# The end of a layer 3 block done in 256-column pieces over the next block's items, with its projection in the bank of the sums, and query evacuations shared by two engines

## The chip, the cores and the metric

The kernel runs on one core of one Trainium2 chip. The metric is the device time of the whole program in microseconds, the median of the timed runs. All data are fp32.

## The reference

Four layers follow each other on an activation `x` of shape (4, 64, 64, 64): four images of 64 x 64 positions (N = 4096) with 64 channels.

```
layer 0: q, k, v = x Wq + bq, x Wk + bk, x Wv + bv         # (B, 4096, 64)
         attn = softmax(q k^T)                              # over j of energy[i, j]
         x = gamma * (attn^T v) + x
layer 1: y = LN(x); y = pointwise 64 -> 256; depthwise 3x3; y1 * y2; channel scale; pointwise 128 -> 64
         x = x + y * beta;  z = LN(x); pointwise 64 -> 256; z1 * z2; pointwise 128 -> 64;  x = x + z * gamma
layer 2: xf = x as (B, 64, 4096), rows are one image axis
         x = softmax(xf^T xf) applied to xf, added to x
layer 3: g, phi, theta = x gW, x phiW, x thetaW             # (B, 4096, 32)
         y = softmax(theta phi^T) g;  w = y W + b           # (B, 4096, 64)
         x = x + gamma * (w - mean(w)) / sqrt(var(w) + eps) + beta   # mean, var over B, H, W
```

## The kernel before

The fast path (`fast_path`) keeps the four images in SBUF as one tile `X` and makes every softmax without a maximum: exps of scores with a constant shift, and sums beside them. At the end `check_sums` (L1635 on) counts whether all sums lie in a safe range and writes a flag; if it is not zero, a general path computes everything again. With the inputs of the reference the flag is zero and only the fast path runs.

The work is written as a list of **items**. An item is a function that issues the scores and exps of one step of the main stream; `at(i, fn)` (L936) puts a function into the list `due` of item i, where it runs after the item's own function. So each engine gets its instructions in the order in which this program is walked through (`run`, L1495 on), and works them off in that order; TensorE, ScalarE and VectorE (here DVE) are under a manual schedule. Beside the items run two **lanes**, `conv` (layer 1 of an image, beside the main stream of later ones) and `misc` (projections, loads, features). A lane is a generator: each `yield us` states after how many us of the main stream's estimated time (3.6 an item of layer 0, 4.6 of layer 2, 1.0 of layer 3) its next piece is issued. The lane's pieces thus fall between items, at places that these numbers set.

The order of the main stream is: layer 0 of images 0 to 3; layer 2 of image 0; then layer 2 of image b followed by layer 3 of image b - 1; at last layer 3 of image 3 directly after layer 3 of image 2.

**Buffers.** `ps` has three PSUM tiles of two banks (128 x 1024) in rotation; all scores, projections and lane products go through them. `acc` has two PSUM tiles of one bank (128 x 512): in layer 3 one holds y, the other (`accz`) the sums z. `e` has six SBUF tiles of 128 x 2048 for the exps, `t` two of 128 x 1024.

**Layer 3** (`layer3`, L1349 on). An image has two blocks (nb = 0, 1) of 2048 queries, and each block has 32 items, one for each 128 keys (mc). In item n:

- `scores(n)`: eight matmuls (L1361) with 32 rows and 64 columns of the array each fill two `ps` tiles, and ScalarE's two exps (L1367) turn them into e(n), 128 x 2048.
- two items later `products(n)`: four matmuls (L1389) add to y in `acc`. The sums of the exps are taken in two ways. In most items DVE adds e(n) to `esum` (L1385; L1383 for the first pair). At mc = 9, 19 and 29 TensorE instead multiplies e(n) by ones into z (four matmuls, L1378). At mc = 31 ScalarE copies y to `yz` (L1395), after both exps that were issued before it.
- two items after that `totals(nb)`: `sums` (L1399) adds esum to z on TensorE; ScalarE makes 1/z as exp(-ln z) (L1410, L1411, 512 columns each); DVE refines it by one Newton step and multiplies y by it (L1412 to L1414).
- four items later `close(nb)`: `project` (L1419) multiplies y by the output weights, four matmuls into a `ps` tile; one ScalarE instruction of 1024 columns adds the bias into `wy` (L1432); DVE takes the batch statistics (L1434).

In the last block of all, `close_last` (L1436 on) does this in halves of 256 columns, with lines L1440 to L1456 in place of those. For the second block of images 0 and 1, whose next items are those of layer 2, `totals` comes directly after the last product.

The features of layer 3 (`open3`: L1315 and its DVE evacuation L1319, L1325 and L1329, L1340 and L1342) and the last scaling of layer 2 (`close2`, L1291 to L1298) run in the misc lane; for image 3 they fall into layer 3 of image 2, its first block.

**Layers 0 to 2.** Layer 0's scores are L1031 with exps L1036, its products L1056, which DVE adds up (L1063). In layer 2 they are L1245, L1253 and L1262. `project0(b)` makes queries and values of the next image within layer 0: for images 1 to 3 (`once`) four matmuls (L982) fill a `ps` tile whose two partition halves DVE evacuates, one after the other, with the bias added (L990, 64 x 1024 each); values go through L1007 and L1009. `norm` (L1077 on) is layer 1's layer norm: ScalarE squares x (L1082), a yield of 4.0, then TensorE sums x and the squares over the channels (L1088). `features2` transposes X for layer 2 (L1224) into a `ps` tile that DVE and ScalarE evacuate (L1227).

**The end.** `finish` computes the batch statistics' scale and shift and stores eight parts of the output. Before the last part's two copies (L1630 on DVE, L1631 on ScalarE) and its store it issues `check_sums`.

## Time and profile before

The device time is 2654.44 us, the median of 3 runs (2654.04 to 2654.82). The profiled execution has a span of 2652.8 us, at a granted TensorE clock of 0.997.

| stretch | what runs | time |
|---|---|---|
| image 0's first layer 3 block | 32 items | 70.88 us |
| image 2's first layer 3 block | 32 items, and image 3's features | 78.38 us |
| image 2's second layer 3 block | 32 items, and the end of the block before | 73.01 us |
| image 3's first layer 3 block | 32 items, and the end of the block before | 73.02 us |

| operation | engine | time of one |
|---|---|---|
| exp of 128 x 1024 (L1367) | ScalarE | 1022 ns |
| add of 128 x 2048 (L1385) | DVE | 2292 ns |
| Ln, Exp of 512 columns (L1410, L1411) | ScalarE | 613, 630 ns |
| bias add of 1024 columns (L1432) | ScalarE | 1133 ns |
| q evacuation of 64 x 1024 (L990) | DVE | 1284 ns |

A busy TensorE in this profile is one with a matmul in flight. Several matmuls on different parts of the array run side by side, so the duration of one says little: a step's cost is read from start to start in the timeline. In a group's line, the numbers after the bar are the busy time in all, the mean of one in ns, and the idle time of the engine just before them with what ended it. In the table by stretch, each engine has its busy time and number of instructions, in the order PE (matmul), PEld (weight load), DVE, ACT (ScalarE), POOL; the last three are the clock, the share of the DMA engines and their GB/s. A timeline line has start, duration, engine, line, operation, and in brackets the idle time before it and what ended it.

### The profile page before, as it was taken

What the parts mean: (1) busy time and instruction counts of PE and PEld (TensorE: products, weight loads), DVE (VectorE), ACT (ScalarE), POOL (GpSimd) and SP (SyncE); (2) the same over time, 40 slices, a digit from 0 to 9 for tenths busy, and PEclk for the clock granted to TensorE, in tenths of its full rate; (3) what the DMA queues carried; (4) which work ended last, traced back from release to release, by engine and by line L of the source; (5) the groups of instructions that cost most, each with busy time, mean ns of one, the idle gap of its engine ahead of it and who ended that gap; (6) DMA issues with size and microseconds to landing.
All of it is one profiled execution on the core that took longest, in us unless ns stands there. A gap on an engine that the chain in (4) does not pass through costs nothing.

```text
span 2652.8 us, 50797 instructions
## 1 busy us (share of the span) xinstructions
PE 2612.8 (98%) x22421; PEld 830.2 (31%) x22421; DVE 1348.6 (51%) x1555; ACT 1718.6 (65%) x2787; POOL 16.4 (1%) x66
## 2 busy tenths in 40 slices
PE   8999999999999999999999999999999999999998
PEld 3333233333323323333333322243322333322223
DVE  3232386633876338621672148800068600098997
ACT  4555655656566565666656668756578755578886
POOL 2000000000000000000000000000000000000000
PEclk9999999999999999999999999999999999999999
DMA  3000000001000100010010000010000010010002
GB/s 73 1 17 1 17 8 10 1 17 25 9 1 1 32 17 1 1 33 17 1 33 17 17 1 1 2 33 1 17 1 2 1 33 1 1 33 2 1 1 66
DMA packets 24282, 36.46 MB, mean 14 GB/s; under 512 B 3725, under 2 KB 12150, under 8 KB 24054
## 3 DMA queue, kind: packets, MB, share of 16 engines
q1 hardware_dynamic: 23141, 32.03, 5.5%
q8 instruction: 178, 2.92, 0.5%
q0 software_dynamic: 672, 0.56, 0.1%
q10 hardware_dynamic: 240, 0.54, 0.1%
q14 instruction: 51, 0.41, 0.1%
HBM read 4.80 MB, written 4.19 MB: 3 GB/s over the span
## 4 chain that ended last, share of the span: by engine, by line
PE 93%; DVE 4%; ACT 2%; issue 0%; DMA 0%; SPq 0%; DVEq 0%; ACTq 0%
PE acc L1056 17%; PE acc L1262 17%; PE ps L1031 17%; PE ps L1245 16%; PE ps L1361 10%; PE acc L1389 8%; PE ps L1118 2%; DVE tg L1385 2%; PE accz L1378 1%; ACT e L1253 1%; PE ps L1209 1%; PE ps L1186 1%; PE ps L1088 1%; PE ps L1340 1%; PE ps L1007 0%
## 5 line engine op out<-in xcount | busy, mean ns | idle before, releaser
L1036 ACT ACTIVATE e<-ps 128x1024 f32<-128x1024 f32 x512 | 517.1, 1025 | 338.1 <-PE ps L1031 225.8
L1253 ACT ACTIVATE e<-ps 128x1024 f32<-128x1024 f32 x512 | 517.0, 1025 | 305.0 <-PE ps L1245 304.9
L1367 ACT ACTIVATE e<-ps 128x1024 f32<-128x1024 f32 x512 | 496.0, 1022 | 85.4 <-PE ps L1361 78.3
L1385 DVE TENSOR_TENSOR tg<-tg,e 128x2048 f32<-128x2048 f32 x214 | 490.4, 2292 | 24.7 <-ACT e L1367 5.7
L1031 PE MATMUL ps<-X,q 64*64 64x512 f32 x4096 | 475.5, 599 | 7.6 <-DVE q L990 4.1
L1245 PE MATMUL ps<-ko 64*64 64x512 f32 x4096 | 469.8, 591 | 2.2 <-ACT ko L1227 1.6
L1262 PE MATMUL acc<-e,X 64*64 64x512 f32 x4096 | 468.5, 591 | 2.6 <-DVE inv L1412 1.6
L1056 PE MATMUL acc<-e,vq 128*64 128x512 f32 x2048 | 467.4, 598 | 0.0
L1063 DVE SCALAR_TENSOR_TENSOR yv<-acc,gam,yv 128x512 f32<-128x512 f32 x224 | 167.8, 750 | 322.6 <-PE acc L1056 311.7
L1157 DVE SCALAR_TENSOR_TENSOR y<-pad,vec,y 128x1024 f32<-128x1024 f32 x240 | 308.1, 1284 | 8.1 <-ACT pad L1141 1.0
L1361 PE MATMUL ps<-tg,ph 32*64 32x512 f32 x4096 | 309.5, 613 | 1.4 <-DVE tg L1329 0.5
L1389 PE MATMUL acc<-e,tg 128*32 128x512 f32 x2048 | 272.0, 603 | 1.5 <-ACT yz L1395 1.5
L1245 PEld LDWEIGHTS ps<-ko 64*64 64x64 f32 x4096 | 157.7, 132 | 288.1 <-issue 195.4
L1262 PEld LDWEIGHTS acc<-e,X 64*64 64x64 f32 x4096 | 159.1, 133 | 278.7 <-issue 263.3
L1031 PEld LDWEIGHTS ps<-X,q 64*64 64x64 f32 x4096 | 143.2, 133 | 323.7 <-issue 224.8
L1056 PEld LDWEIGHTS acc<-e,vq 128*64 128x64 f32 x2048 | 136.0, 136 | 315.1 <-issue 294.4
L1270 DVE TENSOR_TENSOR ph<-ph,acc 128x512 f32<-128x512 f32 x16 | 11.0, 688 | 379.6 <-ACT ph L1269 379.6
L1361 PEld LDWEIGHTS ps<-tg,ph 32*64 32x64 f32 x4096 | 79.5, 129 | 218.7 <-issue 143.2
L1389 PEld LDWEIGHTS acc<-e,tg 128*32 128x32 f32 x2048 | 43.5, 108 | 202.3 <-issue 196.3
L1253 ACT ACTIVATION_READ_ACCUMULATOR e<-ps 128x1 f32 x512 | 106.1, 207 | 0.0
L1036 ACT ACTIVATION_READ_ACCUMULATOR e<-ps 128x1 f32 x512 | 106.0, 207 | 0.0
L1141 ACT ACTIVATE pad<-ps,pwb 128x512 f32<-128x512 f32 x64 | 44.6, 697 | 45.7 <-PE ps L1118 39.0
(193 smaller groups left out, 939.9 us busy)
## 6 DMA issues: line engine op xcount, KB each, us to landing
xn<-t SPq DMA_DIRECT2D x64, 128.0 KB
ph<-tg SPq DMA_DIRECT2D x64, 128.0 KB
ko<-ko SPq DMA_DIRECT2D x16, 256.0 KB
xr<-in_x_dram SPq DMA_DIRECT2D x14, 256.0 KB
q<-q SPq DMA_DIRECT2D x12, 256.0 KB
out_dram<-o SPq DMA_DIRECT2D x5, 512.0 KB
out_dram<-o SPq DMA_DIRECT2D x6, 256.0 KB
xr<-in_x_dram ACTq DMA_DIRECT2D x2, 256.0 KB
```

What stands on the lines that cost most here:

```text
L1031: mm(ps[64 * c : 64 * c + 64, bass.ts(r, 512)], m.q[rows_, 128 * t + 64 * c : 128 * t + 64 * c + 64], x[rows_, bass.ts(g, 512)], start=Tru ...
L1036: act(es[g // 2][:, bass.ts(g % 2, 1024)], ps, AF.Exp, bias=SHIFT0, accum_out=zs[:, g : g + 1],)
L1056: mm(accs[g][64 * r : 64 * r + 64, :], vq, es[half][:, 1024 * g + 512 * r : 1024 * g + 512 * r + 512], start=t == 2 * p, stop=t == 2 * p + 1,)
L1063: stt((x if p == 15 else m.y)[:, cols], accs[g], gam0, (m.y if p else x)[:, cols], ALU.mult, ALU.add,)
L1157: stt(y1, win, wt, y1, ALU.mult, ALU.add)
L1245: mm(ps[64 * c : 64 * c + 64, bass.ts(r, 512)], m.ko[rows_, 128 * jb + 64 * c : 128 * jb + 64 * c + 64], m.ko[rows_, bass.ts(2 * ib + r, 5 ...
L1253: act(es[n, jb], ps, AF.Exp, bias=SHIFT2, accum_out=m.zs[:, jb, ib : ib + 1])
L1262: mm(acc[r][64 * c : 64 * c + 64, :], xw[rows_, jb, :], es[n, jb][rows_, bass.ts(c, 512)], start=jb == 0, stop=jb == 31,)
L1361: mm(tiles[kp][64 * c : 64 * c + 64, bass.ts(i, 512)], m.ph[rows_, 128 * mc + 64 * c : 128 * mc + 64 * c + 64], m.th[rows_, bass.ts(nb, 51 ...
L1367: act(e[:, bass.ts(kp, 1024)], tiles[kp], AF.Exp)
L1385: nc.vector.tensor_add(esum, esum, e)
L1389: mm(st["y"][32 * k : 32 * k + 32, :], m.gx[:, mc, :], e[:, bass.ts(k, 512)], start=mc == 0, stop=mc == 31,)
```

## The change

`spread(n)` replaces `totals` and `close` for a block whose next items belong to layer 3: the first block of every image and the second one of image 2. The inversion is done in 256-column pieces, one after the exps of each of four items, for ScalarE's share of one item to stay small; the Newton step follows. The projection is done in two halves of two matmuls into the bank of the sums z, free by then, so that no `ps` tile is taken from the scores; each half is evacuated in two pieces of 256 columns. As that bank is now in use until item 15 after the block, the next block's first ones product moves from mc = 9 to 13, and the others to 20 and to 27 or 29. In the item in which y is copied, the second exp is held back until behind the copy (`held`), so that y's bank is free sooner.

Apart from layer 3: the second half of a query evacuation goes to ScalarE, so that both halves are read at once; the yield between the squares and the sums of `norm` is 5.0 instead of 4.0; and `check_sums` is issued after the last store instead of before its copies.

```diff
--- before.py
+++ after.py
@@ -987,9 +987,11 @@
                 for o in range(2):
                     own, other = slice(64 * o, 64 * o + 64), slice(64 - 64 * o, 128 - 64 * o)
                     n = bass.ts(2 * j + o, 512)
-                    nc.vector.tensor_scalar_add(
-                        qs[own, :, n], ps[own, :].rearrange("p (s n) -> p s n", s=2), bqk[own, :]
-                    )
+                    src = ps[own, :].rearrange("p (s n) -> p s n", s=2)
+                    if o:
+                        act(qs[own, :, n], src, AF.Identity, bias=bqk[own, :])
+                    else:
+                        nc.vector.tensor_scalar_add(qs[own, :, n], src, bqk[own, :])
                     nc.sync.dma_start(out=qs[other, :, n], in_=qs[own, :, n])
             elif w == "q":
                 for o in range(0, 128, 64):
@@ -1080,7 +1082,7 @@
         sq = [new_t("sq"), new_t("sq")]
         for i in range(2):
             act(sq[i], x[:, bass.ts(i, 1024)], AF.Square)
-        yield 4.0
+        yield 5.0
         ps = new_ps()
         for i, src in enumerate(((x, x), (sq[0], sq[1]))):
             for j in range(4):
@@ -1301,6 +1303,8 @@
 
 
     wys, early = {}, []
+    small = {}
+    held = []
 
     def open3(b):
         x, m = X[:, b], im[b]
@@ -1363,21 +1367,27 @@
                             m.ph[rows_, 128 * mc + 64 * c : 128 * mc + 64 * c + 64],
                             m.th[rows_, bass.ts(nb, 512)], start=True, stop=True,
                         )
-            for kp in range(2):
-                act(e[:, bass.ts(kp, 1024)], tiles[kp], AF.Exp)
+            for fn in small.get((first + n, "PE"), []):
+                fn()
+            act(e[:, 0:1024], tiles[0], AF.Exp)
+            held.append(lambda: act(e[:, 1024:2048], tiles[1], AF.Exp))
+            if not (mc == 1 and (nb or last)):
+                held.pop()()
+            for fn in small.get((first + n, "ACT"), []):
+                fn()
 
         def products(n):
             nb, mc = n // 32, n % 32
             e, esum = es[n], m.tg[:, 2048:4096]
             if mc == 0:
                 st["y"] = new_acc()
-            if mc % 10 == 9 or (last and n >= 62):
-                if mc == 9:
+            if mc in (13, 20, 27 if n < 61 else 29) or (last and n >= 62):
+                if mc == 13:
                     st["z"] = new_acc("accz")
                 for k in range(4):
                     mm(
                         st["z"][32 * k : 32 * k + 32, :], ones[:, 0:32], e[:, bass.ts(k, 512)],
-                        start=mc == 9, stop=False,
+                        start=mc == 13, stop=False,
                     )
             elif mc == 1:
                 nc.vector.tensor_add(esum, es[n - 1], e)
@@ -1393,6 +1403,8 @@
             if mc == 31 and not (last and n == 63):
                 st["yz"] = new_t("yz")
                 nc.scalar.copy(st["yz"][:, 0:512], st["y"])
+                if held:
+                    held.pop()()
 
         def sums():
             for k in range(4):
@@ -1401,17 +1413,26 @@
                     m.tg[:, 2048 + 512 * k : 2560 + 512 * k], start=False, stop=True,
                 )
 
-        def totals(nb):
-            sums()
-            yz, z = st["yz"], st["z"]
-
-            t = new_t("inv")
+
+        def invert(cols):
+            t = st["inv"] = st.get("inv") or new_t("inv")
+            act(t[:, cols], st["z"][:, cols], AF.Ln)
+
+        def invert2(cols):
+            act(st["inv"][:, cols], st["inv"][:, cols], AF.Exp, scale=-1.0)
+
+        def newton(nb):
+            yz, z, t = st["yz"], st["z"], st.pop("inv")
             r, d = t[:, 0:512], t[:, 512:1024]
-            act(r, z, AF.Ln)
-            act(r, r, AF.Exp, scale=-1.0)
             nc.vector.tensor_mul(d, z, r)
             stt(d, d, -2.0, r, ALU.add, ALU.mult, accum_out=inv3[:, 2 * b + nb : 2 * b + nb + 1])
             stt(yz[:, 0:512], d, -1.0, yz[:, 0:512], ALU.mult, ALU.mult)
+
+        def totals(nb):
+            sums()
+            invert(slice(0, 512))
+            invert2(slice(0, 512))
+            newton(nb)
 
         def project(yz, ps, c0, cols):
             for k in range(4):
@@ -1421,11 +1442,47 @@
                     yz[32 * k : 32 * k + 32, cols], start=True, stop=True,
                 )
 
-        def close(nb):
+        def open_wy(nb):
             if b % 2 == 0 and nb == 0:
                 wys["pair"] = new_big("wy") if b else new_pad("wy")
             if nb == 0:
                 wys[b] = wys["pair"][:, bass.ts(b % 2, 2048)]
+
+        def project_half(nb, jj):
+            if jj == 0:
+                open_wy(nb)
+            for s in range(2):
+                k = 2 * s + jj
+                mm(
+                    st["z"][64 * s : 64 * s + 64, :], wo[32 * k : 32 * k + 32, :],
+                    st["yz"][32 * k : 32 * k + 32, 0:512], start=True, stop=True,
+                )
+
+        def take(nb, jj, i):
+            wy = wys[b][:, 1024 * nb + 512 * jj + 256 * i : 1024 * nb + 512 * jj + 256 * i + 256]
+            act(wy, st["z"][:, bass.ts(i, 256)], AF.Identity, bias=V("L3_conv_w_b"))
+            if i:
+                nc.vector.bn_stats(
+                    bst[:, b, nb, jj, :], wys[b][:, 1024 * nb + 512 * jj : 1024 * nb + 512 * jj + 512]
+                )
+
+
+        def spread(n):
+            nb = n // 32
+            at(first + n + 4, sums)
+            for m, kind, fn in (
+                (5, "ACT", lambda: invert(slice(0, 256))), (6, "ACT", lambda: invert(slice(256, 512))),
+                (7, "ACT", lambda: invert2(slice(0, 256))), (8, "ACT", lambda: invert2(slice(256, 512))),
+                (9, "ACT", lambda: newton(nb)),
+                (12, "PE", lambda: project_half(nb, 0)), (12, "ACT", lambda: take(nb, 0, 0)),
+                (13, "ACT", lambda: take(nb, 0, 1)),
+                (14, "PE", lambda: project_half(nb, 1)), (14, "ACT", lambda: take(nb, 1, 0)),
+                (15, "ACT", lambda: take(nb, 1, 1)),
+            ):
+                small.setdefault((first + n + m, kind), []).append(fn)
+
+        def close(nb):
+            open_wy(nb)
             ps = new_ps()
             project(st["yz"], ps, 512, slice(0, 512))
             wy = wys[b][:, bass.ts(nb, 1024)]
@@ -1460,9 +1517,11 @@
             at(first + n + 2, lambda n=n: products(n))
             if last and n == 63:
                 at(first + n + 2, close_last)
+            elif n == 63 and b < 2:
+                at(first + n + 2, lambda: totals(1))
+                at(first + n + 8, lambda: close(1))
             elif n % 32 == 31:
-                at(first + n + (2 if n == 63 and b < 2 else 4), lambda n=n: totals(n // 32))
-                at(first + n + 8, lambda n=n: close(n // 32))
+                spread(n)
 
 
     conv_from, misc_from, misc_to = {}, {}, {}
@@ -1626,10 +1685,10 @@
             if i < 2 * B - 1:
                 nc.scalar.copy(os[i][:, 0:1024], pss[i])
             else:
-                check_sums(mv)
                 nc.vector.tensor_copy(os[i][:, 0:512], pss[i][:, 0:512])
                 nc.scalar.copy(os[i][:, 512:1024], pss[i][:, 512:1024])
             store(i, os[i])
+        check_sums(mv)
 
 
     def check_sums(mv):
```

## The prediction

> **What bounds the kernel.** I read part 1 of the page first, then its costliest groups.

> ```profile
> PE 2612.8 (98%) x22421; PEld 830.2 (31%) x22421; DVE 1348.6 (51%) x1555; ACT 1718.6 (65%) x2787; POOL 16.4 (1%) x66
> L1367 ACT ACTIVATE e<-ps 128x1024 f32<-128x1024 f32 x512 | 496.0, 1022 | 85.4 <-PE ps L1361 78.3
> L1385 DVE TENSOR_TENSOR tg<-tg,e 128x2048 f32<-128x2048 f32 x214 | 490.4, 2292 | 24.7 <-ACT e L1367 5.7
> ```

> TensorE is busy 98% and the chain that ended last is 93% TensorE. Here TensorE has no slack to fill: what adds matmuls there costs time, and what removes a TensorE wait gains. In layer 3 ScalarE is nearly as full (two exps of 1.02 us an item, idle 85.4 us over 256 items).

> Second view: the busy time by stretch, from the first product of a block of 32 items to that of the next. The rows are image 0's first block, image 2's first, image 2's second, and image 3's first.

> ```profile
> 1562.97:1633.85 70.88, 70.57 (x796) 15.78 (x793) 63.14 (x28) 61.87 (x66) 0.00 (x0) 1.00 0.01 2
> 2325.23:2403.61 78.38, 77.10 (x860) 19.81 (x856) 72.00 (x42) 61.87 (x66) 0.00 (x0) 1.00 0.13 28
> 2403.61:2476.62 73.01, 72.70 (x808) 16.25 (x808) 65.18 (x34) 64.30 (x69) 0.00 (x0) 1.00 0.01 1
> 2476.62:2549.64 73.02, 72.67 (x809) 16.25 (x809) 67.04 (x34) 64.35 (x69) 0.00 (x0) 1.00 0.01 2
> ```

> A block with another block's end inside takes 73.0, one without 70.9: the end costs 2.1 us. Third view, TensorE's timeline at such an end, and at a ones product:

> ```profile
> 1644.17 1.63 PE L1361 MATMUL ps<-tg,ph 32*64 32x512 f32 x16
> 1645.62 1.09 PE L1419 MATMUL ps<-yz,wo 32*64 32x512 f32 x8
> 1646.64 1.07 PE L1389 MATMUL acc<-e,tg 128*32 128x512 f32 x8
> 1647.64 1.11 PE L1361 MATMUL ps<-tg,ph 32*64 32x512 f32 x16
> 1648.68 1.07 PE L1389 MATMUL acc<-e,tg 128*32 128x512 f32 x8
> ...
> 1655.13 1.06 PE L1378 MATMUL accz<-e,ones 128*32 128x512 f32 x8
> 1656.01 1.04 PE L1389 MATMUL acc<-e,tg 128*32 128x512 f32 x8
> ```

> Start to start: an item is 2.04 us here, the projection 1.02, a ones product 0.88. Items elsewhere alternate 2.04 and 2.20 (mean 2.12), the longer one waiting for an exp to free a score buffer. So of the 2.1 us of a block end, 1.02 + 0.88 (the sums) are matmuls; waits are only some 0.2, plus about 0.2 for the copy of y just before.

> Fourth, TensorE waits longer than 0.5 us, looked up one by one. Layers 0 to 2 have some 10 us of them. The largest, the one at a norm, and the DVE work behind the first:

> ```profile
> 403.95 1.09 PE L1031 MATMUL ps<-X,q 64*64 64x512 f32 x8 [3.15 <-DVE q L990]
> 1159.40 2.00 PE L1088 MATMUL ps<-sq,jsel 128*32 128x512 f32 x8 [1.62 <-ACT sq L1082]
> ...
> 401.30 2.59 DVE L990 TENSOR_SCALAR q<-ps,bqk 64x1024 f32<-64x1024 f32 x2
> ```

> [...] the trace has 0.88 for four ones products side by side. [...] eight score matmuls take 1.04 us, four projection matmuls 1.02. Two should therefore take nearly as long as four. [...] The trace has 0.38 and 0.60 (the Ln of the last and of the other blocks), so halving a piece saves only about 0.22. [...] The bubbles at block ends here are only 0.4 us each.

> **The change part by part.** Spread ends are five: the first block of each image, and the second of image 2.

> *More ones products.* The condition on mc is true at 13, 20, 27 and 29 in every second block (items 59 and 61), so four where there were three; the instruction order confirms 120 matmuls against 104. That is 4 x 0.87 = +3.5 us. The vector add it saves (2.3 us) is off the path, since ScalarE waited for an ordinary L1385 add nowhere in the trace. At the very end it counts: TensorE waits 0.5 us for the last add before the sums, and this goes. -0.5.

> *Projection in two halves.* Two products of two matmuls at 0.88 instead of one of 1.02: +0.74 x 5 = +3.7.

> *New waits.* The second half overwrites the bank that the second wy piece is read from, which stands on ScalarE behind the exps of the item before. From the start of that item's scores: exps end at 3.09, the piece at about 3.5, while TensorE is at the half at 3.1. It waits about 0.45, with that item's products and the next scores queued behind it. The next block's first ones product, one item after the last piece, waits the same way for about 0.4. Some 0.1 goes into the item's own slack, leaving 0.75 against the roughly 0.33 that the old projection lost (1643.63, ScalarE waiting 0.76 for the late add). 5 x 0.42 = +2.1.

> *Inversion in four pieces.* Ln and Exp of 512 took 1.18 together, in the item where the sums (0.88 on TensorE) gave ScalarE room, and cost 0.1. Now four pieces follow in the next four items, each 0.31 to 0.35 between exp pairs of 1.95. ScalarE needs 2.28 an item against 2.12. Going through these items with the score buffers' release, TensorE loses about 0.6. 5 x 0.5 = +2.5.

> *The held exp.* The copy of y runs one exp earlier, so the new y no longer waits (0.3); the exp behind it is 0.5 later and holds a score buffer. I put this at 0, from -0.3 to +0.3 each.

> *First ones product at 13 instead of 9.* In image 2's first block layer 2's last scaling and layer 3's features use DVE; that block takes 78.38. The features' buffer waits behind DVE adds:

> ```profile
> 2349.04 4.68 DVE L1385 TENSOR_TENSOR tg<-tg,e 128x2048 f32<-128x2048 f32 x2
> 2353.64 1.28 DVE L1319 TENSOR_SCALAR tg<-ps,vec 128x1024 f32<-128x1024 f32 x1
> ...
> 2353.43 1.06 PE L1389 MATMUL acc<-e,tg 128*32 128x512 f32 x8
> 2354.97 1.12 PE L1361 MATMUL ps<-tg,ph 32*64 32x512 f32 x16 [0.48 <-DVE tg L1319]
> ```

> Item 9 now adds on DVE, so three adds stand ahead, not two. L1319 starts at 2353.64 + 2.34 = 2356.0 and ends at 2357.2; TensorE, 0.88 earlier without the ones product, wants the buffer at 2353.6 and waits 3.6 instead of 0.5. The ones product follows at 13 and the second such wait (0.5) goes: the block is about 2.6 longer.

> *Query evacuations.* Half goes to ScalarE, which is idle 3 us around 403. DVE gets to its second half after 1.3 us less of the first, with two adds of 1.28 instead of one plus the 1.41 pair ahead: it ends at about 401.75 rather than 403.89, -2.1. The two waits of images 1 and 3 (0.4, 1.15) shrink by 0.4 and 0.85. Sum -3.4.

> *Yield 5 instead of 4 before the norm's sums.* In the new order the squares of the norm at 1157 stand ahead of four exps, not behind: -1.8. None of the other seven gets that pattern. The layer 1 work behind shifts one slot; at image 0's layer 2 features two buffers are now held just before scores: +0.9 (a wait of 1.1 becoming 2.0).

> *The check after the last store.* DVE's last copy could start 0.85 earlier. But the DMA engines are full (share 0.93 or more) from 2640 to 2648, and the flag comes 2 us later, with loads and branches behind it. 0, from -0.8 to +1.5.

> Sum: 3.5 - 0.5 + 3.7 + 2.1 + 2.5 + 2.6 = +13.9 in layer 3; -3.4 - 1.8 + 0.9 = -4.3 before it. Together +9.6: 2654.4 + 9.6 = 2664.0.

> **The rivals.** *No change* (0.27): TensorE's 0.08 us of slack an item and the room that its own added matmuls give ScalarE hide the new waits, the pieces and the features' buffer. Only the matmuls stay: +6.7 - 4.3 = +2.4, 2656.8. For it: the old inversion cost only 0.1. Against: that slack is what the items use to wait for each other.

> *Faster* (0.14): the halves run beside the scores, on two of eight tiles, and cost 0.2 each. Then 5 x (0.4 - 1.02) = -3.1, +3.5 for the ones products, -2.2 for the old waits at the ends, and -8 of the 10 us in layers 0 to 2, as the new spacing resolves more of them: -9.8, 2644.6. Against: products on all 128 rows follow each half, and a shifted lane makes new waits as easily.

> *Much slower* (0.07): DVE, with its end work between adds, comes late enough that exps wait for an e buffer, or the shifted layer 1 meets new waits: +18, 2672. By my count of six buffers, adds may run 8.4 us late and run at most 6.7 late.

> **How the numbers follow.** My main case has 0.52: 2664.0. Leaving out the two outer rivals, 0.21, the range is 2651 (the main sum with every uncertain term low, and some of the no-change case with a larger early gain) to 2669 (waits half as large again). Faster by over 0.2% 0.14, within 0.2% 0.27, slower 0.59.

> **What would show it.** Right: second blocks with a spread end at about 75.5 us instead of 73.0; four ones products of 0.88 in each; the halves at 0.9 each, the second and the next ones product after a wait for wy; ScalarE without idle over the four pieces; the stretch of image 2's first block near 81 with a wait of 3 us or more on the theta evacuation; the wait at 404 near 1 us and the one at 1159 gone. Wrong: halves that cost under 0.5, blocks of 73 or less, or a layer 0 to 2 stage over 7 us shorter.

## The result, and the profile after

The changed kernel takes **2678.07 us** (median of 6 runs, 2677.14 to 2678.76), the kernel before 2655.14 us on the same chip: a ratio of 1.0086, 95% interval 1.0073 to 1.0099. It is slower by about 22.9 us. The prediction was 2664.0 us with a range to 2669: the direction held, the size did not.

The two profiled executions differ by as much, 2652.8 and 2676.2 us. First the page of the changed kernel: the busy times of the engines, and the groups that answer to the exp and the vector add of before.

```profile
PE 2629.4 (98%) x22453; PEld 836.2 (31%) x22453; DVE 1331.7 (50%) x1545; ACT 1726.4 (65%) x2818; POOL 16.4 (1%) x66
...
L1395 DVE TENSOR_TENSOR tg<-tg,e 128x2048 f32<-128x2048 f32 x210 | 481.1, 2291 | 29.8 <-ACT e L1373 12.4
...
L1372 ACT ACTIVATE e<-ps 128x1024 f32<-128x1024 f32 x256 | 263.0, 1027 | 99.6 <-PE ps L1365 81.7
```

TensorE has 16.6 us more busy time, with nearly as many instructions. The added ones products and the split projections were forecast at 3.5 and 3.7 us of it, so some 9 us are neither. Where they are, the stretches tell. The columns are the stretch and its length, the busy time of PE, PEld, DVE, ACT and POOL, then the granted clock; the rows are those of before: image 0's first block, image 2's first and second, image 3's first.

```profile
1571.88:1642.42 70.54, 70.54 (x797) 15.81 (x793) 63.15 (x28) 61.41 (x65) 0.00 (x0) 1.00 0.01 2
2338.50:2421.85 83.35, 79.61 (x860) 20.14 (x857) 72.09 (x42) 61.39 (x65) 0.00 (x0) 0.96 0.12 27
2421.85:2496.95 75.10, 74.72 (x821) 17.21 (x817) 64.81 (x33) 64.44 (x74) 0.00 (x0) 1.00 0.01 1
2496.95:2571.18 74.23, 73.85 (x812) 16.93 (x809) 67.37 (x34) 64.43 (x74) 0.00 (x0) 1.00 0.01 2
```

The first row starts at 1571.88 where before it started at 1562.97, although every line of the change that is about layer 3 comes later: **8.9 us are lost before layer 3 begins**, where the prediction had a gain of 4.3. Laying all blocks side by side (time from a block's first product to that of the next; the second blocks of images 0 and 1 run on into the next image's layer 2):

| kernel | start of layer 3 | image 0 | | image 1 | | image 2 | | image 3 | | after it |
|---|---|---|---|---|---|---|---|---|---|---|
| before | 1562.97 | 70.88 | 311.92 | 70.89 | 308.57 | 78.38 | 73.01 | 73.01 | 71.24 | 31.94 |
| after | 1571.88 | 70.53 | 314.32 | 70.53 | 311.24 | 83.35 | 75.09 | 74.23 | 73.06 | 31.97 |
| difference | +8.9 | -0.35 | +2.40 | -0.36 | +2.67 | +4.97 | +2.08 | +1.22 | +1.82 | 0.0 |

Layer 3 adds 14.5 us, where the prediction had 13.9, and the tail nothing, as forecast. Image 2's first block alone is far from its term (2.6). In these rows the column behind the busy times says 0.96 for this block: its TensorE did not always have its full clock. The granted clock around each long TensorE wait of the changed kernel shows where. First the waits, TensorE's lines with the last releaser in brackets:

```profile
402.53 3.25 PE L1033 MATMUL ps<-X,q 64*64 64x512 f32 x16 [3.51 <-ACT q L992]
...
743.95 3.22 PE L1033 MATMUL ps<-X,q 64*64 64x512 f32 x16 [1.97 <-ACT pad L1143]
...
1054.73 1.78 PE L1264 MATMUL acc<-e,X 64*64 64x512 f32 x5 [2.13 <-DVE X L1065]
...
1338.55 1.92 PE L1319 MATMUL ps<-X,thw 64*32 64x512 f32 x4 [2.79 <-DVE X L1300]
...
2370.64 2.02 PE L1365 MATMUL ps<-tg,ph 32*64 32x512 f32 x16 [3.74 <-DVE tg L1323]
```

Then the stretches of 4 us that hold the work after each of them:

```profile
402.00:406.00 4.00, 3.47 (x20) 0.96 (x24) 0.66 (x1) 3.87 (x8) 0.38 (x3) 0.64 0.63 135
744.00:748.00 4.00, 4.00 (x24) 1.14 (x24) 0.00 (x0) 3.68 (x7) 0.00 (x0) 0.57 0.01 4
1054.00:1058.00 4.00, 3.27 (x14) 1.35 (x18) 3.96 (x7) 0.00 (x0) 0.00 (x0) 0.64 0.01 4
1338.00:1342.00 4.00, 3.45 (x15) 0.74 (x19) 3.10 (x4) 1.38 (x2) 0.39 (x3) 0.57 0.00 0
2370.00:2374.00 4.00, 3.36 (x24) 0.73 (x28) 2.79 (x2) 1.31 (x2) 0.00 (x0) 0.50 0.02 4
```

After each of these waits TensorE runs at half its clock (over these 4 us it was granted 0.50 to 0.64): 16 score matmuls take 3.2 us at 402 and 744, where the same 16 take 1.9 elsewhere. Summed over windows of 2 us, (1 - clock) x time is 1.7 us at each of the first four waits and 3.4 us at the last. Of the last, 0.7 us is no loss of its own: for 1.4 us of the half clock TensorE still waited. In the kernel before, the same windows show one such place apart from the first 60 and the last 40 us, behind the wait at 404. So the new losses hold 6.9 us in the three waits of 2 to 2.8 us before layer 3, 5.1 in the half clock behind them, and some 2.7 in the half clock behind the wait in image 2's first block; a wait of 1.62 us at the norm at 1157 is gone. With 1.7 us of half clock behind it, a wait of 1.97 us cost nearly twice what its line shows, and the second half of that stands under busy time.

A loss of 1.7 us at half clock is a slow stretch of 3.4 us. The waits ahead of the five are 1.97 to 3.74 us long; their length alone does not decide, since runs further on have a wait of 1.97 us and one of 3.01 with no slow stretch behind. What goes with it is worked out in the last section.

Who the waits wait for is the next question. At 402 it is ScalarE's half of the queries, and the view of waits says for whom that half waited (us in total, times, longest):

```profile
ACT q L992 <- DVE q L994: 15.7, 6, 6.3
```

All six halves of ScalarE sat waiting for VectorE's half of the same tile. At 402 the timeline has them one after the other:

```profile
400.07 1.27 DVE L994 TENSOR_SCALAR q<-ps,bqk 64x1024 f32<-64x1024 f32 x1
...
401.37 1.11 ACT L992 ACTIVATE q<-ps,bqk 64x1024 f32<-64x1024 f32 x1 [6.26 <-DVE q L994]
402.50 1.02 ACT L1038 ACTIVATE e<-ps 128x1024 f32<-128x1024 f32 x1
```

ScalarE was idle for 6.26 us and started when VectorE ended, with its own four exps queued behind. Each of the six L992 in the trace carries a wait on VectorE's semaphore, which neither the diff nor the order of instructions shows.

### The profile page after: what moved, and what is told of

Same layout as the page of the kernel before. It is cut to its first block, busy times and chain, and to the rows that moved or that the text cites. A ratio compares the mean times of both kernels' runs of the same rounds, so it can differ in the third digit from the quotient of the medians.

```text
span 2676.2 us, 50862 instructions
## 1 busy us (share of the span) xinstructions
PE 2629.4 (98%) x22453; PEld 836.2 (31%) x22453; DVE 1331.7 (50%) x1545; ACT 1726.4 (65%) x2818; POOL 16.4 (1%) x66
## 4 chain that ended last, share of the span: by engine, by line
PE 93%; DVE 4%; ACT 2%; issue 0%; DMA 0%; SPq 0%; POOL 0%; DVEq 0%; POOLq 0%
PE acc L1058 17%; PE ps L1033 17%; PE acc L1264 16%; PE ps L1247 15%; PE ps L1365 10%; PE acc L1399 9%; PE ps L1120 2%; DVE y L1159 1%; PE accz L1388 1%; DVE tg L1395 1%; PE ps L1009 1%; PE ps L1211 1%; PE ps L1188 1%; PE ps L1344 1%; PE ps L1090 1%
## 5 line engine op out<-in xcount | busy, mean ns | idle before, releaser
L1038 ACT ACTIVATE e<-ps 128x1024 f32<-128x1024 f32 x512 | 517.1, 1025 | 306.0 <-PE ps L1033 218.8
L1255 ACT ACTIVATE e<-ps 128x1024 f32<-128x1024 f32 x512 | 517.0, 1025 | 302.9 <-PE ps L1247 302.8
L1395 DVE TENSOR_TENSOR tg<-tg,e 128x2048 f32<-128x2048 f32 x210 | 481.1, 2291 | 29.8 <-ACT e L1373 12.4
L1372 ACT ACTIVATE e<-ps 128x1024 f32<-128x1024 f32 x256 | 263.0, 1027 | 99.6 <-PE ps L1365 81.7
L1373 ACT ACTIVATE e<-ps 128x1024 f32<-128x1024 f32 x256 | 261.7, 1022 | 0.0
```

The costliest lines, as they stand in the source:

```text
L1038: act(es[g // 2][:, bass.ts(g % 2, 1024)], ps, AF.Exp, bias=SHIFT0, accum_out=zs[:, g : g + 1],)
L1255: act(es[n, jb], ps, AF.Exp, bias=SHIFT2, accum_out=m.zs[:, jb, ib : ib + 1])
L1372: act(e[:, 0:1024], tiles[0], AF.Exp)
L1373: held.append(lambda: act(e[:, 1024:2048], tiles[1], AF.Exp))
L1395: nc.vector.tensor_add(esum, esum, e)
```

## The experiments

**Theory:** before layer 3, the loss is the 5.0 ahead of the norms' sums. It moves all of layer 1 and the second convolution by a slot, and three times the moved work stands ahead of something that TensorE needs; and the shared queries gain nothing since their halves are read one after the other. In layer 3 the terms of the prediction hold, but for the half clock. **Rivals:** ScalarE's query halves make the waits; or the halves and the shift are harmless and the waits come from an interplay with the layer 3 part.

### The parts one at a time

Queries alone: the diff's first hunk on the kernel before.

> The kernel before with only the query evacuations shared (second half of each tile on ScalarE). Theory now (the two halves are read one after the other[...]): TensorE's wait at 404 us stays above 3 us with about 4 us at half clock behind it, ScalarE's halves each start when VectorE's end, and the time is 2653 to 2658. My prediction's step (halves side by side, -3.4 us): the wait at 404 is near 1 us without the slow stretch and the time is 2650 to 2652. Layer 3 is as before in both.

Measured: 2654.50 against 2654.51 us, ratio 1.000 (0.9991 to 1.0008). The wait at 402 stays (3.64 us, for L992), each L992 waits for L994 (15.8 us in six times), and layer 3 starts at 1563.05. The gain that I had forecast is absent, and the rival that makes the query halves the cause of the loss falls.

The 5.0 alone:

```
-        yield 4.0
+        yield 5.0
```

> The kernel before with only the 5.0 instead of 4.0 ahead of the norm's sums. Theory now (the shift by one slot brings new TensorE waits of 2 to 2.8 us near 741, 1053 and 1335 us, each with some 3.4 us at half clock behind it, against 3.6 us gained at the norm at 1157): 2660 to 2664. Rival (those waits come from ScalarE's new query halves and not from the shift): the norm's gain of 2 to 4 us alone, 2650 to 2653. My prediction's step: -0.9 us, 2654.

Measured: 2661.83 us, ratio 1.0028 (1.0018 to 1.0038); layer 3 starts at 1570.43, 7.5 us late. All three new waits are there, of 1.97, 2.13 and 2.80 us, each with a slow stretch. How a moved piece makes one shows at image 0's features, in the lines of VectorE and TensorE. The kernel before:

```profile
1331.06 0.68 DVE L1296 TENSOR_TENSOR ph<-ph,rz 128x512 f32<-128x512 f32 x1
1331.78 0.69 DVE L1298 TENSOR_TENSOR X<-X,ph 128x512 f32<-128x512 f32 x1
1332.97 1.92 PE L1315 MATMUL ps<-X,thw 64*32 64x512 f32 x16
```

And with the 5.0:

```profile
1333.02 2.60 DVE L1157 SCALAR_TENSOR_TENSOR y<-pad,vec,y 128x1024 f32<-128x1024 f32 x2
1335.53 0.68 DVE L1296 TENSOR_TENSOR ph<-ph,rz 128x512 f32<-128x512 f32 x1
1336.25 0.69 DVE L1298 TENSOR_TENSOR X<-X,ph 128x512 f32<-128x512 f32 x1
...
1337.00 1.92 PE L1315 MATMUL ps<-X,thw 64*32 64x512 f32 x4 [2.80 <-DVE X L1298]
```

Two convolution steps (2.60 us) now stand ahead of the last scaling of X, and the features' last four matmuls wait 2.80 us for it. The one at 1053 is the same on image 3's last update of layer 0 (L1063 behind six convolution steps). At 741 it is ScalarE: the pointwise evacuation L1141 waits 5.20 us for the clearing of its pad, with the exps behind it. Its line in this run:

```profile
740.67 1.42 ACT L1141 ACTIVATE pad<-ps,pwb 128x512 f32<-128x512 f32 x2 [5.20 <-POOL pad L1133]
```

From item to item, TensorE's starts lose 3.6 us at the first, 3.5 at the second and 7.0 over two items at the third, and gain 3.6 at the norm at 1157. These differences also hold lane pieces that only moved to a neighbouring item (one item after the norm, 1.9 of its 3.6 are gone again), so they are not to be added. The terms do add up: 6.9 us of waits and 5.1 of half clock, less 2.8 for the norm by itself (measured below), less 1.7 because in this run the wait at 404 (3.01 us) has no slow stretch behind it, make 7.5. That last term is not the edit's; the last section shows where it comes from.

The changed kernel with the layer 3 of before (queries, 5.0, and the check of the sums behind the last store):

> The changed kernel with layer 3 as before: shared query evacuations, the 5.0, and the check of the sums after the last store. Theory now: all of the loss before layer 3 is here, layer 3 starts 8 to 10 us later than before and the time is 2662 to 2665, with the waits near 741, 1053 and 1335 us. My prediction's sum for these parts: -4.3 us, 2650. Rival (the loss in the first layers comes only together with the layer 3 part, since ends of image 1 and 3 lie in them): no more than 2 us, 2655 or less.

Measured: 2661.53 us, ratio 1.0026 (1.0016 to 1.0036), layer 3 at 1569.90: the 5.0 alone comes to as much, and the other two parts are worth nothing within the noise. The remaining 2.0 us to the changed kernel's 1571.88 are mostly the half clock behind the wait at 741, which here has the same length (1.97 us) and no slow stretch.

The layer 3 part alone:

> The kernel before with the layer 3 part alone: spread ends, projections in halves, the fourth ones product, the held exp. Theory (its terms were right but for image 2's first block, where a wait of nearly 4 us is followed by some 7 us at half clock): +13 to +16 us, 2667 to 2671, with image 2's first block at 83 us. Rival (most of the loss is the clock over the whole kernel or an interplay with the first layers): +7 us or less, 2662 or less.

Measured: 2668.74 us, ratio 1.0056 (1.0039 to 1.0072). Its eight blocks are together 14.5 us longer than those of before, as in the changed kernel, with image 2's first block at 83.45. So the loss in layer 3 and the one ahead of it are separate, and the rival of an interplay falls.

### Mending the two parts before layer 3

Queries shared by whole tiles, so that no tile has two readers (`if j:` in place of `if o:`):

```
-                    if o:
+                    if j:
                         act(qs[own, :, n], src, AF.Identity, bias=bqk[own, :])
```

> The kernel before with the query evacuations shared by whole tiles: the first tile of an image on VectorE, the second on ScalarE, so that no tile is read by both engines and the built program has no wait of ScalarE for VectorE there. Theory (the hand-off within a tile is what ate the gain of the change's form): the wait near 400 us falls to 2 us or less, the slow stretch behind it goes with it, and the time is 2 to 5 us below the kernel before, 2649.5 to 2652.5. Rival (ScalarE's 2.2 us ahead of its exps cost as much as VectorE's): the wait at 400 stays above 3 us or moves to the exps, 2653 to 2656.

Measured: 2650.69 us, ratio 0.9988 (0.9981 to 0.9994); layer 3 starts 4.0 us earlier than before. In its timeline ScalarE's tile goes through as soon as it is written:

```profile
397.20 2.24 ACT L992 ACTIVATE q<-ps,bqk 64x1024 f32<-64x1024 f32 x2 [5.89 <-PE ps L982]
...
399.50 1.09 PE L1033 MATMUL ps<-X,q 64*64 64x512 f32 x8 [0.65 <-ACT q L992]
```

The wait is 0.65 us instead of 3.64 with the halves, and the slow stretch is gone. By the medians the gain is 3.1 us. So the hand-off within a tile ate the gain. Whether two engines can read the halves of one tile side by side, no run here shows.

The 5.0 at the second norm of image 2 alone, and one less behind it so that nothing later moves:

```
-    def norm(x, y):
+    def norm(x, y, us=4.0):
...
-        yield 4.0
+        yield us
...
-        yield 5.0
+        yield 9.0 - us
...
-        yield from norm(x, z)
+        yield from norm(x, z, 5.0 if b == 2 else 4.0)
```

> The kernel before with the 5.0 ahead of the sums of one norm alone (the second of image 2, at 1157 us), and one less behind it, so that nothing later is shifted. Theory (the 3.6 us gained there in the changed kernel is from the order of the squares and exps at this norm; the loss is from the shift of everything else): 2650 to 2652, the wait at 1157 gone and no new wait near 740, 1052 or 1335 us. Rival (the gain belongs to the whole shift): within 1 us of the kernel before.

Measured: 2651.54 us, ratio 0.9991 (0.9982 to 0.9999), 2.2 us by the medians; in the trace layer 3 starts 3.4 us earlier (2.8 of it at this norm), without any of the three waits. The norm's gain is real and separate from the shift.

### Taking the layer 3 part to pieces

Three ones products in every block:

```
-            if mc in (13, 20, 27 if n < 61 else 29) or (last and n >= 62):
+            if mc in (13, 20, 27 if nb == 0 else 29) or (last and n >= 62):
```

> The layer 3 part alone, with three ones products in every block (items 13, 20, 27 in first blocks and 13, 20, 29 in second ones). By my prediction's term the four dropped products are 0.87 us each: 3.5 us under the layer 3 part alone, near 2665.2. Rival (the product stood in a place where TensorE waited anyway, or the add that takes its place makes ScalarE or TensorE wait): 1 us or less, 2668 or more.

Measured: 2663.56 us, ratio 1.0037 (1.0024 to 1.0051). The four second blocks are 0.85, 0.83, 0.91 and 0.85 us shorter than in the layer 3 part alone, 3.4 together. (Image 2's first block is 1.05 shorter too, with a shorter stretch at half clock behind the same wait: 1.7 us lost there instead of 3.4.)

Image 2's first block with its first ones product at 9:

```
+            z0 = 9 if b == 2 and nb == 0 else 13
...
-            if mc in (13, 20, 27 if n < 61 else 29) or (last and n >= 62):
-                if mc == 13:
+            if mc in (z0, 20, 27 if n < 61 else 29) or (last and n >= 62):
+                if mc == z0:
...
-                        start=mc == 13, stop=False,
+                        start=mc == z0, stop=False,
```

> The layer 3 part alone, with image 2's first block taking its ones products at 9, 20 and 27 instead of 13, 20 and 27, so that two adds instead of three stand ahead of the features' evacuation on VectorE. Theory (the wait of nearly 4 us at 2357 and the 3.4 us or more at half clock behind it come from the third add): the block falls from 83 to about 78.5 us, the time by 4 to 5 us to 2664 to 2665. My prediction's term: 2.6 us, 2666. Rival (the wait comes from the end of the block before or the held exp): no change, 2668.7.

Measured: 2662.84 us, ratio 1.0031 (1.0019 to 1.0043). The block falls from 83.45 to 77.97: the third add costs 5.5 us. In the changed kernel VectorE had three adds ahead of the features' evacuation:

```profile
2362.32 7.08 DVE L1395 TENSOR_TENSOR tg<-tg,e 128x2048 f32<-128x2048 f32 x3
2369.31 1.28 DVE L1323 TENSOR_SCALAR tg<-ps,vec 128x1024 f32<-128x1024 f32 x1
```

With the product at 9 it has two, and TensorE waits 0.48 us as it did before the change:

```profile
2354.59 4.68 DVE L1394 TENSOR_TENSOR tg<-tg,e 128x2048 f32<-128x2048 f32 x2
2359.19 1.28 DVE L1321 TENSOR_SCALAR tg<-ps,vec 128x1024 f32<-128x1024 f32 x1
...
2360.52 1.12 PE L1363 MATMUL ps<-tg,ph 32*64 32x512 f32 x16 [0.48 <-DVE tg L1321]
```

With both mends, the projection whole again, in a score buffer, while the pieces of the inversion and the held exp stay:

```
             at(first + n + 4, sums)
+            at(first + n + 10, lambda: close(nb))
...
-                (12, "PE", lambda: project_half(nb, 0)), (12, "ACT", lambda: take(nb, 0, 0)),
-                (13, "ACT", lambda: take(nb, 0, 1)),
-                (14, "PE", lambda: project_half(nb, 1)), (14, "ACT", lambda: take(nb, 1, 0)),
-                (15, "ACT", lambda: take(nb, 1, 1)),
```

> The layer 3 part alone with three ones products in every block (at 9 in image 2's first) and the projection whole again, in a score buffer of its own two items after the inversion, instead of in two halves in the bank of the sums; the inversion in four pieces and the held exp stay. Theory (what is left of the layer 3 loss, 14 less 3.5 for the fourth products and 5 for image 2's first block, is the halves and the waits around them, 1.16 us an end by my prediction's terms): 5.5 to 6 us less, that is within 1.5 us of the kernel before, 2653 to 2655.5. Rival (it is the pieces of the inversion on ScalarE, 0.5 us an end in my prediction, or more): 3 to 6 us above the kernel before, 2657 to 2660.

Measured: 2659.25 us, ratio 1.0019 (1.0011 to 1.0026), the value of the rival, but for another cause. What TensorE waited for ahead of the projection, by the answer on its line (us, times):

```profile
  DVE yz L1428: 5.0, 4
```

Four of the five projections waited, 1.54 to 1.59 us each, for the last step of the inversion (L1428), which the pieces had moved to just before them. (The line counts three of these and a short one; the fourth is put down to an exp, but there too L1428 ended 0.1 us ahead of the projection. The 2.1 us in the next expectation is too high.) The run had a wait of its own and decided nothing, so the projection was moved two items on:

```
-            at(first + n + 10, lambda: close(nb))
+            at(first + n + 12, lambda: close(nb))
```

> The run with the whole projection, its projection moved two items further (12 items after the block instead of 10). There the trace showed TensorE waiting 2.1 us at four of five projections for VectorE's last step of the inversion. Theory (the pieces of the inversion and the held exp cost nothing, and what is left of the layer 3 loss is the halves): the waits go, some 7 us less, 2651.5 to 2654, about the kernel before. Rival (the pieces cost 0.5 us an end, as my prediction had it): 2655 to 2657.

Measured: 2651.63 us, ratio 0.9988 (0.9982 to 0.9995), **faster than the kernel before**. Its end has the inversion in pieces and no wait around the projection:

```profile
1651.57 1.21 PE L1363 MATMUL ps<-tg,ph 32*64 32x512 f32 x16
1652.60 1.09 PE L1439 MATMUL ps<-yz,wo 32*64 32x512 f32 x8
1653.62 1.07 PE L1398 MATMUL acc<-e,tg 128*32 128x512 f32 x8
```

The changed kernel, at the same place of the same block:

```profile
1661.67 1.21 PE L1365 MATMUL ps<-tg,ph 32*64 32x512 f32 x16
1662.58 1.16 PE L1456 MATMUL accz<-yz,wo 32*64 32x512 f32 x4
1663.67 1.06 PE L1399 MATMUL acc<-e,tg 128*32 128x512 f32 x8
...
1666.70 1.33 PE L1365 MATMUL ps<-tg,ph 32*64 32x512 f32 x16
1668.22 1.07 PE L1456 MATMUL accz<-yz,wo 32*64 32x512 f32 x4 [0.19 <-ACT wy L1463]
...
1672.27 1.28 PE L1365 MATMUL ps<-tg,ph 32*64 32x512 f32 x16
1673.73 1.07 PE L1388 MATMUL accz<-e,ones 128*32 128x512 f32 x8 [0.19 <-ACT wy L1463]
```

A half takes as long as the whole: from its start to that of the next matmul 1.08 and 1.00 us in all five ends, against 1.02 (each product counts twice in these lines, so x4 is a half and x8 the whole). The second half waits 0.19 us for the first half's last wy piece, and the ones product 0.19 for the second's. By the blocks of the last run and of the one before the projection was made whole (less 0.83 to 0.91 for each fourth product, as measured above), halves with their waits cost 1.40, 1.80, 1.51, 1.43 and 1.50 us an end, 7.6 in all. Of this 1.06 an end, 5.3 in all, is the second half itself. What is left of the layer 3 part in the last run (pieces, held exp, the ones products' new places) makes, with the projection four items later than before, the eight blocks 2.1 us shorter than before.

### Do the terms stand side by side?

The changed kernel with the four mends (whole tiles, the one norm, three products, 9 in image 2's first block), halves of the projection still in:

> The changed kernel with the four mends together: queries shared by whole tiles, the 5.0 at the one norm alone, three ones products in every block, and at 9 in image 2's first. If the terms stand side by side: layer 3 starts at 1555.4 us less the held exps' nothing, 16.5 earlier than in the changed kernel, and is 3.5 + 5.4 shorter, 2652 to 2654.5. Rival (the mends of layer 3 and of the first layers hide one another): 2657 or more.

Measured: 2653.49 us, ratio 0.9997 (0.9988 to 1.0006), some 24 us under the changed kernel, with layer 3 at 1556.56.

The kernel before with whole tiles and the one norm, then with the held exp as well:

> The kernel before with the queries shared by whole tiles and the 5.0 at the one norm. If the two gains stand side by side: 2.9 + 2.3 to 3.6 us, 2647.5 to 2649. Rival (the shorter queries move the lanes so that the norm loses its place again): 2650 to 2651.

> The same with the held exp of the change alone (the copy of y ahead of the second exp of the next block's second item), without any other part of its layer 3. Theory (the held exp gives the 0.36 us that image 0's and 1's first blocks lost in the changed kernel, at five block ends): 1 to 2 us below the run without it, 2646 to 2648. My prediction's step: 0, from -1.5 to +1.5.

Measured: 2647.69 us, ratio 0.9976 (0.9967 to 0.9985), and 2646.64 us, ratio 0.9972 (0.9961 to 0.9983). In the traces the held exp gives 0.36 to 0.38 us in the first blocks of images 0 to 2, 0.25 in each of the next two and loses 0.1 in each of the others, a gain of 1.2 us in all; over the kernel the two intervals overlap.

Since a ones product is 0.87 us of TensorE, I tried two instead of three in all blocks but image 2's first, and then with the second at 29:

```
-            if mc % 10 == 9 or (last and n >= 62):
...
+            three = b == 2 and nb == 0
+            z0 = 9 if three else 13
+            if mc in ((9, 19, 29) if three else (13, 27)) or (last and n >= 62):
```

> The same with two ones products (items 13 and 27) instead of three in every block but image 2's first, and the vector add in their place. Theory (a ones product is 0.87 us of TensorE, which has no slack, and the add is 2.3 us of VectorE, which has some in these blocks): seven products fewer, 6 us less, 2640 to 2642. Rival (VectorE, at 64 to 65 us of a 71 to 73 us block, comes late and exps or the end wait): less than 3 us gained, or slower than the run with three, 2645 or more.

> The run with two ones products, the second at item 29 instead of 27, so that two adds instead of four stand between it and the block's sums, where the trace of that run showed TensorE waiting 2 to 3.3 us for VectorE's last add, with a slow stretch behind. Theory (VectorE falls behind 0.17 us an add, and the ones product near the end catches it up): 3 to 6 us below the run with three products, 2641 to 2644. Rival (VectorE cannot carry 29 adds in a block that also holds another block's end): 2647 or more.

Measured: 2656.79 us, ratio 1.0009 (1.0002 to 1.0016), and 2655.59 us, ratio 1.0005 (0.9996 to 1.0013): 9 to 10 us slower than with three. The first blocks of images 0 and 1 gain 0.8 each; four of the others lose 3.5 to 4.5 in the first of the two runs, for the reason put down as the rival's:

```profile
2462.33 16.67 DVE L1392 TENSOR_TENSOR tg<-tg,e 128x2048 f32<-128x2048 f32 x7
...
2479.05 1.49 PE L1408 MATMUL accz<-tg,ones 128*32 128x512 f32 x8 [2.75 <-DVE tg L1392]
```

In a block with another block's end inside, VectorE comes late, and the sums wait for its last add, with half clock behind (1.7 us lost behind this wait of 2.75). Moving the product to 29 left waits of 2.43, 2.43 and 2.95 us.

Last, everything that gained: whole tiles, the one norm, the late whole projection with pieces and held exp, two ones products in those two first blocks alone.

> Everything that gained, together: queries shared by whole tiles and the 5.0 at the one norm; the changed kernel's held exp and inversion in pieces with the whole projection at item 12; ones products at 13, 20 and 27 or 29, at 9 in image 2's first block, and only two (13, 27) in the first blocks of images 0 and 1, which hold no other block's end. If the gains stand side by side: 2654.4 less 6.5 for the first layers, 2.8 for layer 3 and 1.7 for two products, 2643 to 2645. Rival (they overlap, or the two products bring a late add): 2646 or more.

Measured: **2644.83 us, ratio 0.9964 (0.995 to 0.9978)**, faster than both kernels, near the sum of the parts. Over the run with the held exp (0.9972) the intervals overlap, so a further gain from the layer 3 part is not shown. Its page:

```profile
PE 2608.2 (99%) x22405; PEld 829.3 (31%) x22405; DVE 1345.0 (51%) x1551; ACT 1723.1 (65%) x2803; POOL 16.4 (1%) x66
```

## Why the prediction was wrong

The sum had -4.3 us before layer 3 and +13.9 in it. Layer 3 came to +14.5. **What failed is the part before layer 3: +8.9.**

*Yield 5 instead of 4* (-1.8 and +0.9). This is the step that failed most. I looked the norms through for the one pattern that gains, "None of the other seven gets that pattern", and charged the shift with one wait, becoming 2.0. The gain was there and larger (2.8 us in the trace of its own run, 2.2 by the medians), and the wait that I charged did not grow (0.84 us at 918 in the run with the 5.0 alone, 0.93 before). But the shift moves every convolution step and pointwise evacuation behind it, and I did not follow these against what TensorE needs at 741, 1053 and 1335. Three waits of 2.0, 2.1 and 2.8 us came of it, with 1.7 us of half clock each: 12.0 where I had 0.9. Less the norm's 2.8 this is 9.2, against the 8.9 measured. My *much slower* rival named this ("the shifted layer 1 meets new waits") and was given 0.07.

*Query evacuations* (-3.4): 0. I counted VectorE's shorter half and took ScalarE's as beside it. They are one after the other. In the form where they are not, the gain is 3.1 us by the medians. That this is near my figure is luck: in its trace the gain is all at 404 (2.5 of wait and 1.7 of half clock), and the wait of image 3 that was to shrink by 0.85 is 1.03 us where it was 0.98.

*First ones product at 13* (+2.6). The mechanism was right to the detail: three adds ahead, a wait of 3.6 forecast and 3.74 found. The size was not: 5.5 by the run that takes the third add out (4.97 in the changed kernel's block, to which the held exp gives back 0.4), as the wait is followed by half clock, which costs some 2.7 us on top of it. No term of mine had the clock in it. I had seen the same pattern in the trace of before, at 404, and counted only the 3.15 us of its wait.

*Fourth ones products* (+3.5): 3.4. *Projection in halves with its waits* (3.7 + 2.1): 7.6, since a half keeps TensorE as long as a whole, 1.04 us on average and not 0.88: 5.3 of the 7.6, where I had 3.7. My own reading, that two products take nearly as long as four, said so; the term used the figure of a ones product. That leaves 2.3 for the waits, close to their term. *Inversion in pieces, held exp and the end's wait* (2.5 + 0 - 0.5): -2.1. ScalarE's pieces cost TensorE nothing: the items that hold them take 2.11 to 2.14 us, the mean of other items being 2.12. The held exp alone gave 1.2. So the layer 3 sum was near by luck: two groups of terms were too small by 1.8 and 2.9 us, and one too large by 4.1. *The check after the last store* (0): 0, the tail is 31.97 us against 31.94.

## What to carry to other kernels

A change of spacing in a lane of work that shares engines with a full TensorE has to be followed down to every later place where TensorE waits for these engines, not only to the place that it was made for; a shift for one place alone is the safer form, and here it gained while the general one lost. Price a TensorE wait of two microseconds or more with the half clock behind it, 1.7 us here in most cases, which shows as busy time and not as a wait; whether it came went here with how the wait lay on a grid of 3.413 us (next section), so the same wait of 1.97 us cost it in two runs and not in a third. Before counting two engines as sharing one tile's evacuation, look whether the built program lets them: by whole tiles it gained 0.12%, by halves nothing.

## What the runs showed of the hardware

The same wait need not cost the same. In the run with the second ones product at 29, TensorE waited 2.43 us for VectorE's last add in two blocks:

```profile
2474.19 1.94 PE L1408 MATMUL accz<-tg,ones 128*32 128x512 f32 x8 [2.43 <-DVE tg L1392]
...
2550.04 1.07 PE L1408 MATMUL accz<-tg,ones 128*32 128x512 f32 x8 [2.43 <-DVE tg L1392]
```

The eight matmuls behind it took 1.94 us the first time and 1.07 the second. So it was with the wait of 1.97 us at 741: half clock behind it in the changed kernel and in the run with the 5.0 alone, none in the run without the layer 3 part. And the wait of the kernel before at 404, 3.0 to 3.15 us, has a slow stretch behind it in six of the eight traces that keep it, but none in those of the 5.0 alone and of the late whole projection.

```profile
2470.22:2473.63 3.41, 1.54 (x16) 0.33 (x16) 3.31 (x2) 3.15 (x4) 0.00 (x0) 1.00 0.00 0
2473.63:2477.04 3.41, 2.85 (x16) 0.59 (x16) 0.51 (x1) 0.82 (x2) 0.00 (x0) 0.50 0.00 0
...
2545.31:2548.72 3.41, 2.30 (x24) 0.41 (x16) 3.31 (x2) 3.41 (x5) 0.00 (x0) 1.00 0.00 0
2548.72:2552.14 3.42, 2.10 (x24) 0.65 (x32) 1.26 (x1) 1.43 (x3) 0.00 (x0) 1.00 0.00 0
```

The first wait has 1.87 us in one step, and the next step runs at half clock; the second is divided, 1.11 and 1.32 us, and no step behind it does. At 404 the two traces without a slow stretch divide TensorE's idle time 1.53 and 1.91, and 1.77 and 1.80 us; in the kernel before it is 1.49 and 2.08. Over all 18 traces, without the first 60 and the last 40 us, each of the 21 steps at full clock in which TensorE was idle for 1.97 us or more was followed by half clock, and none with less than 1.4 us was; from 1.4 to 1.91 us both occur. (The ends of matmuls are modelled in these records, so the border is no sharper than that.) In image 2's first block the wait of 3.74 us reached 1.42 us into its slow step, and a second slow one followed. So in these traces some 2 us of idle time in one step of 3.413 us were enough, and 3.57 us divided 1.77 and 1.80 over two steps were not. What sets the steps, no run here shows.
